# Two heads of layer 0 side by side, their sums on GpSimd, and three steps of layer 1 moved

## The chip, the cores and the metric

One core of a Trainium2 chip runs the whole network in one launch. The metric is the device time of that launch in microseconds, the median of three runs. All data are float32.

## The reference, cut to what matters

Four images of 32 x 32 positions and 384 channels pass through four layers with residual connections. Only the first two matter here (`_gn` is a group norm):

```python
# layer 0, on _gn(x): 6 heads of 64 channels; each query sees its own bias map
q = x @ w_q + b_q                                   # 1024 positions
xs = bilinear sample of x at learned positions      # 1024 samples per head group
k, v = xs @ w_k + b_k, xs @ w_v + b_v
bias = bilinear sample of rpe at (query - position) # 1024 x 1024 per head
attn = softmax(q @ k.T * 64**-0.5 + bias)           # over the 1024 keys
x = x + (attn @ v) @ w_out + b_out

# layer 1, on _gn(x): 12 heads of 32 channels
sim  = sigmoid(beta + alpha * l2norm(xg) @ l2norm(gc).T)  # 1024 x 256 per head
gw   = (sim @ sim.T) * gamma + (1 - gamma)                # 1024 x 1024
attn = softmax(q @ k.T * 32**-0.5) * gw
attn = attn / (attn.sum(keys) + 1e-8)
x = x + (attn @ v) @ Wproj
```

Layers 2 (box filters) and 3 (an attention over 3 x 3 neighbourhoods) follow.

## The kernel before

**Two streams of work.** `Front` computes layer 0 of an image, `Trunk` layers 1 to 3. Both are Python generators that yield weights for the work they have just emitted. `Net.layer3` advances the trunk of image b and, keeping step by these weights (`TRUNK_STEPS` 1109, `FRONT_STEPS` 714), the front of image b + 1. So the front of images 1 to 3 is interleaved with the trunk of images 0 to 2. Image 0's front runs alone at the beginning, and image 3's trunk runs alone at the end. Image 0's heads have code of their own, `heads0`, whose order is pinned by hand.

**Who sets the order.** A scheduling layer takes the emitted instructions, orders each engine's queue by when it expects their inputs, and puts in the waits. Tiles come from pools by tag: `self.wt(shape, tag, bufs)` gives one of `bufs` buffers, and a new tile waits until the last reader of that buffer is done. Engines work through their queues in order, so an instruction that waits holds up all behind it. PSUM has two pools: `bank()` gives one of four tiles of 512 columns, and `big()` one of two tiles of 1024 columns.

**Layer 0's heads, images 1 to 3 (`head0`).** One call handles one head `h` and one half `q` of the queries (512 of them), so there are 12 calls per image. In each, eight blocks `j` of 128 keys are done. For each block:

- an indirect DMA, issued by GpSimd (POOL), gathers a bias window `win` (L830);
- ScalarE (ACT) and VectorE (DVE) interpolate it in y and x: L842, L843, L847, L848, giving `lg`;
- TensorE (PE) multiplies keys and queries (L851). The keys of a head have 64 channels; they lie in `kz`, whose other 64 rows are zero, so that the matmul takes both heads' queries and all 128 rows;
- DVE adds it to `lg` (L852) and keeps a running maximum `rmax` (L855, L857).

Then PE transposes the maxima, DVE reduces them (L868), POOL spreads them on a diagonal (L870), PE broadcasts that (L872) and ACT copies it to `tb` (L876). For each block again, DVE subtracts `tb` (L883), ACT takes the exponential (L884), and PE multiplies with the values `va` into 64 rows of the bank `po`, and with a block of ones into the other 64 rows, which gives the sums (L886). `over_sums` divides after each two heads. The pool of `lg` has 13 buffers of 512 columns.

**Layer 1 (`pair`).** Six calls per image, each for two heads, with eight steps `j` over blocks of 128 keys. In a step:

- POOL scales a slice of the similarities into `sg` (L1492, two buffers);
- PE computes logits with keys and queries of two heads in 64-row tiles (L1509), ACT exponentiates them into `e` (L1517);
- PE multiplies similarities (L1539), or transposes parts that an earlier step had (L1534);
- DVE multiplies this with `e` and sums (L1546); ACT keeps parts for later (L1551);
- PE multiplies with the scaled values (L1481) into `av`.

Beside this runs a pre-pass for the next pair: `sums_step` computes logits in four 32-row tiles (L1382) into two `big` tiles; DVE takes the maximum (L1390) and ACT exponentiates and sums (L1391). `sums_finish` makes the row constants (logarithm on DVE, a transposition on PE, L1416), which are stored and loaded as an extra row of `qa` (`load_lse`). `sims` computes the next pair's similarities (L1429, ACT L1437, DVE L1440). At the end of a pair `av` is copied to `y` (L1569) and stored. The copies of `y` mark the ends of the pairs in the trace.

The core of the emission order in a step, before:

```python
            for h in range(2):          # e of both halves is emitted above
                for r in range(2):      # products, then DVE's multiply (L1546)
                    ...
                if h == 0 and st:
                    for i in (0, 1) if j == 0 else (j + 1,):
                        if i < NJ:
                            self.sums_step(i, st)
                if st and j == NJ - 1:
                    self.sims(h)
            ...
            if st and j == NJ - 2:
                self.sums_finish(p + 1, st)
                self.load_lse(p + 1)
```

Of the kernel before, what the change touches and what calls it, by code (L numbers as in the profile page):

```python
# [20 lines left out]
AF = mybir.ActivationFunctionType  # L21
# [51 lines left out]
class Net:  # L73
# [132 lines left out]
    def scratch(self):  # L206
# [13 lines left out]
        self.k0 = dram("k0", [C, N])  # L220
        self.gcd = dram("gcd", [C, M1])
# [204 lines left out]
class Front(Lane):  # L426


    def layer0(self, b):
        nc, v = self.nc, self.nc.vector  # L430
        with self.scope("l0"):
# [3 lines left out]
            self.kz = [self.wt([P, N], f"kz{r}") for r in range(2)]  # L435
            for r in range(2):
                nc.gpsimd.memset(self.kz[r][GC * (1 - r) : GC * (2 - r), :], 0.0)
            self.va = self.wt([P, NJ, C], "va")
            self.f = self.wt([P, 2, 2, NJ * G], "bias_f")
            self.widx = self.wt([P, 2, NJ * G], "widx", 1, I32)  # L440
            if b == 0:

                self.side = "left"
                with self.scope("l0f"):
                    self.side = "right"
                    self.heads = self.heads0(self.work)
# [9 lines left out]
            with self.scope("l0b"):  # L456
                self.load_keys(0)
                for h in range(G):
                    if h + 1 < G:
                        self.load_keys(h + 1)  # L460
                    for q in range(2):
                        yield from self.head0(h, q)
                    if h % 2:
                        yield from self.over_sums(h // 2)
# [166 lines left out]
    def inputs0(self, b):  # L631
# [145 lines left out]
        va, bv = self.va, self.rows[:, R_BV0 : R_BV0 + C]  # L777
# [3 lines left out]
        def value(j):  # L781
            v.tensor_tensor(va[:, j, :], self.dense_n(xsT, w, j), bv, ALU.add)
# [32 lines left out]
    def head0(self, h, q):  # L815

        nc, v = self.nc, self.nc.vector
        f, kz, va = self.f, self.kz[h % 2], self.va
        k, r0 = h // 2, (h % 2) * GC
        rows = slice(r0, r0 + GC)  # L820
        other = slice(GC - r0, 2 * GC - r0)
        HH, HN = HW // 2, N // 2
        both = self.qpad[:, k, 1 + HH * q : 1 + HH * (q + 1), 1 : 1 + HW]
        queries = both[rows]
        logits = []
        rmax = self.wt([P, HN], "rmax", 2)
        for j in range(NJ):
            c = j * G + h
            win = self.wt([P, (HH + 1) * WROW], "win", 4)
            nc.gpsimd.indirect_dma_start(  # L830
                out=win,
                out_offset=None,
                in_=self.strips[:, :],
                in_offset=bass.IndirectOffsetOnAxis(
                    ap=self.widx[:, q, c : c + 1], axis=0
                ),
            )
            wv = win.rearrange("p (r c) -> p r c", c=WROW)
            sc = lambda i, t: f[:, i, t, c : c + 1]

            z = self.wt([P, HH, HW + 1], "z", 3)
            nc.scalar.activation(z, wv[:, 0:HH, 0 : HW + 1], AF.Copy, scale=sc(1, 1))  # L842
            v.scalar_tensor_tensor(  # L843
                z, wv[:, 1 : HH + 1, 0 : HW + 1], sc(0, 1), z, ALU.mult, ALU.add
            )
            lg = self.wt([P, HH, HW], "lg", 13)
            nc.scalar.activation(lg, z[:, :, 0:HW], AF.Copy, scale=sc(1, 0))  # L847
            v.scalar_tensor_tensor(lg, z[:, :, 1 : HW + 1], sc(0, 0), lg, ALU.mult, ALU.add)  # L848
            lf = lg.rearrange("p y x -> p (y x)")
            ps = self.bank()  # L850
            nc.tensor.matmul(ps, kz[:, j * P : (j + 1) * P], both, start=True, stop=True)  # L851
            v.tensor_tensor(lf, ps, lf, ALU.add)  # L852
            logits.append(lf)
            if j == 1:
                v.tensor_tensor(rmax, logits[0], lf, ALU.max)  # L855
            elif j > 1:
                v.tensor_tensor(rmax, rmax, lf, ALU.max)  # L857
            yield 3


        NI = HN // P
# [19 lines left out]
        for j in range(NJ):  # L881
# [5 lines left out]
            if j % 2:  # L887
                yield 2
# [1038 lines left out]
```

## Time and profile before

| | |
|---|---|
| Time of three runs | 4602.47, 4607.11 and 4614.23 us, median 4607.11 |
| Span of the profiled execution | 4578.1 us, 47313 instructions |
| Outside the span, against the median | 29.0 us |
| Mean granted TensorE clock | 0.948 |
| First `y` copy to the sixth, image 0's trunk | 850.1 to 1459.4 us |
| First `y` copy to the sixth, image 3's trunk | 4042.4 to 4426.9 us |

The profile gives the profiled execution's time as its span, from its first instruction to its last; its device time is not given apart from that, so the difference to the median stands for what lies around the span.

The span is long because everything is done for four images, and because two streams share the engines. A stretch of time in which image 0's trunk runs beside image 1's heads is repeated, nearly alike, for the next two images, some 1112 us later each time (the first `y` copies are at 850.1, 1963.0 and 3075.8 us). The groups of instructions give, for each line, engine and operation, a count of records, the busy time and the mean of one. A float32 matmul leaves two records. The busy time of a group counts overlapping records once, so the busy time divided by the number of matmuls is a better price than the mean duration of a record.

### The profile page before, as it was taken

To read this page: it belongs to the slowest core of one execution; us is meant where nothing else is said; L and a number is where in the kernel's file an instruction comes from. 1 tells how busy PE (TensorE), PEld (TensorE's weight loads), DVE (VectorE), ACT (ScalarE), POOL (GpSimd) and SP (SyncE) were. 2 spreads that over 40 slices of the span, in tenths; PEclk is the share of its full clock that TensorE was granted. 3 is DMA by queue.
4 is the path that set the end of the run, shared out by engine and by line. 5 is a ranking of instruction groups with operands and counts; after the bars stand their busy time and mean duration, and the time that the engine had idled before them with its cause. 6 is when DMAs were issued, how large, how long until landed. Compare 5 with 4: busy or idle time off the path is not lost.

```text
span 4578.1 us, 47313 instructions
## 1 busy us (share of the span) xinstructions
PE 4150.6 (91%) x15896; PEld 1795.0 (39%) x15896; DVE 3138.6 (69%) x5909; ACT 2303.6 (50%) x3633; POOL 972.6 (21%) x994
## 2 busy tenths in 40 slices
PE   5699889999999898999999989899999998999998
PEld 2333334333334443433333444343333335344444
DVE  4599466878787628687878744678786884566654
ACT  2266334667664314465666422456665641555632
POOL 1644123212111104211212110522120211000000
PEclk8799989999999898999999989899999998999998
DMA  6444234212121245321212134432121213311011
GB/s 139 150 144 129 79 125 123 64 52 84 51 59 55 86 114 164 93 55 39 84 50 79 38 105 125 135 103 66 45 71 36 72 38 123 105 32 27 20 41 42
DMA packets 232852, 371.01 MB, mean 81 GB/s; under 512 B 117763, under 2 KB 165728, under 8 KB 232608
## 3 DMA queue, kind: packets, MB, share of 16 engines
q1 hardware_dynamic: 180568, 201.26, 15.4%
q0 software_dynamic: 39936, 145.53, 10.8%
q10 hardware_dynamic: 12104, 21.19, 1.4%
q8 instruction: 126, 2.06, 0.2%
q14 instruction: 118, 0.97, 0.1%
HBM read 287.90 MB, written 80.27 MB: 80 GB/s over the span
## 4 chain that ended last, share of the span: by engine, by line
PE 56%; DVE 14%; ACT 7%; issue 5%; DMA 4%; POOL 2%; SPq 0%; ACTq 0%; DVEq 0%; POOLq 0%
PE bank L1539 13%; PE big L1509 5%; PE big L1382 4%; PE bank L851 4%; PE big L403 4%; PE bank L886 4%; PE bank L417 4%; PE bank L1534 3%; PE bank L1481 3%; DVE nmax L1390 2%; DVE e L1546 2%; PE bank L1219 2%; PE big L666 2%; PE big L1664 1%; POOL gat L738 1%
## 5 line engine op out<-in xcount | busy, mean ns | idle before, releaser
L1539 PE MATMUL bank<-whole,sg 128*128 128x512 f32 (+3 forms) x2304 | 852.5, 505 | 7.0 <-POOL sg L1492 7.0
L1546 DVE SCALAR_TENSOR_TENSOR e<-bank,gam,e 128x512 f32<-128x512 f32 x768 | 561.9, 747 | 349.2 <-PE bank L1539 226.7
L1391 ACT ACTIVATE big<-big,nmax 128x1024 f32<-128x1024 f32 x384 | 417.6, 1087 | 322.3 <-DVE nmax L1390 322.1
L1517 ACT ACTIVATE e<-big 128x1024 f32<-128x1024 f32 x384 | 379.7, 1019 | 363.2 <-PE big L1509 362.1
L1539 PEld LDWEIGHTS bank<-whole,sg 128*128 128x128 f32 x2304 | 403.4, 197 | 369.6 <-issue 281.6
L1390 DVE TENSOR_REDUCE nmax<-big 128x1 f32<-128x1024 f32 x384 | 454.5, 1219 | 76.4 <-PE big L1382 75.9
L830 POOL DMA_INDIRECT win<-strips,widx x288 | 316.2, 1098 | 658.0 <-DVE z L843 391.8
L1492 POOL TENSOR_SCALAR sg<-whole,gam 128x512 f32<-128x512 f32 x192 | 143.7, 750 | 1442.6 <-PE bank L1539 1019.6
L1509 PE MATMUL big<-qa,ka 64*128 64x512 f32 x1536 | 417.8, 630 | 9.7 <-ACT big L1391 9.5
L1382 PE MATMUL big<-k,q 32*128 32x512 f32 x1536 | 327.7, 674 | 82.2 <-ACT big L1391 45.2
L738 POOL DMA_INDIRECT gat<-pairs,sidx x192 | 209.2, 1090 | 378.8 <-DVE ix_gt L519 217.4
L851 PE MATMUL bank<-qpad,kz 128*128 128x512 f32 x576 | 278.8, 613 | 9.4 <-ACT gf L1551 9.4
L886 PE MATMUL bank<-lg,va 128*64 128x512 f32 x576 | 265.6, 605 | 15.0 <-ACT lg L884 14.9
L886 PE MATMUL bank<-lg,ones 128*64 128x512 f32 x576 | 265.0, 605 | 0.0
L848 DVE SCALAR_TENSOR_TENSOR lg<-z,bias_f,lg 128x512 f32<-128x512 f32 x288 | 213.7, 759 | 47.4 <-ACT lg L847 45.7
L1509 PEld LDWEIGHTS big<-qa,ka 64*128 64x128 f32 x1536 | 135.7, 188 | 256.3 <-issue 124.3
L842 ACT ACTIVATE z<-win,bias_f 128x528 f32<-128x528 f32 x288 | 202.9, 735 | 55.4 <-DVE lg L848 34.4
L852 DVE TENSOR_TENSOR lg<-bank,lg 128x512 f32<-128x512 f32 x288 | 192.9, 685 | 49.4 <-PE bank L851 48.1
L883 DVE TENSOR_TENSOR lg<-lg,tb 128x512 f32<-128x512 f32 x288 | 191.5, 710 | 46.9 <-ACT tb L876 46.9
L843 DVE SCALAR_TENSOR_TENSOR z<-win,bias_f,z 128x528 f32<-128x528 f32 x288 | 215.5, 772 | 11.3 <-ACT z L842 9.8
L1481 PE MATMUL bank<-e,vs 128*32 128x512 f32 x1536 | 206.7, 604 | 3.9 <-DVE vs L1475 3.9
L847 ACT ACTIVATE lg<-z,bias_f 128x512 f32<-128x512 f32 x288 | 200.0, 716 | 12.0 <-PE bank L886 6.1
(314 smaller groups left out, 6620.8 us busy)
## 6 DMA issues: line engine op xcount, KB each, us to landing
pairs<-xn SPq DMA_DIRECT2D x64, 192.0 KB
q<-qd SPq DMA_DIRECT2D x48, 256.0 KB
w<-in_gmat SPq DMA_DIRECT2D x16, 576.0 KB
w<-in_w_off SPq DMA_DIRECT2D x12, 576.0 KB
w<-in_Wqkv SPq DMA_DIRECT2D x12, 576.0 KB
a<-in_x SPq DMA_DIRECT2D x16, 384.0 KB
x<-a ACTq DMA_DIRECT2D x4, 1536.0 KB
res<-x SPq DMA_DIRECT2D x12, 512.0 KB
```

Of the source, the lines that this page charges most:

```text
L738: nc.gpsimd.indirect_dma_start(out=gat[:, g].rearrange("p l c -> p (l c)"), out_offset=None, in_=pairs[:, :], in_offset=bass.IndirectOffse ...
L830: nc.gpsimd.indirect_dma_start(out=win, out_offset=None, in_=self.strips[:, :], in_offset=bass.IndirectOffsetOnAxis(ap=self.widx[:, q, c : ...
L851: nc.tensor.matmul(ps, kz[:, j * P : (j + 1) * P], both, start=True, stop=True)
L886: nc.tensor.matmul(po[out, :], w, lf, start=j == 0, stop=j == NJ - 1)
L1382: nc.tensor.matmul(ps[r][:, h * 512 : (h + 1) * 512], self.q4[rows, i * P : (i + 1) * P], self.k4[rows, 0:512], start=True, stop=True,)
L1390: v.tensor_reduce(nmax[:, r, i : i + 1], ps[r], AX.X, ALU.max, negate=True)
L1391: nc.scalar.activation(ps[r], ps[r], AF.Exp, bias=nmax[:, r, i : i + 1], accum_out=den[:, r, i : i + 1],)
L1481: nc.tensor.matmul(av[r0 : r0 + HD1, :], vs[:, r, :], es[h][:, r, :], start=j == 0, stop=j == NJ - 1,)
L1509: nc.tensor.matmul(ps[:, r, :], ka[rows, j * P : (j + 1) * P], qa[rows, cols], start=True, stop=True,)
L1517: nc.scalar.activation(e, ps, AF.Exp)
L1539: nc.tensor.matmul(ps[:, (mid - i0) * P :], sg[:, r, m, :], sim[:, h, r, m, (mid - i0) * P :], start=m == 0, stop=m == 1,)
L1546: v.scalar_tensor_tensor(e[:, r, :], ps, self.gam[:, 1:2], e[:, r, :], ALU.add, ALU.mult, accum_out=tot[:, r, h : h + 1],)
```

## The change

Line numbers in this section are given for the kernel before.

**Layer 0, images 1 to 3.** `two_heads(k, q)` takes the place of two calls of `head0`. It handles heads 2k and 2k + 1 together. Keys of both heads are loaded as one tile of 128 rows without zeros. Their logits are two matmuls of 64 rows each, into the two halves of one `big` tile. The four interpolation instructions stay 512 wide for each head; the addition, maximum, subtraction and exponential become 1024 wide. Values of two heads go into the two 64-row halves of `po`, each with its own exponentials. The sums over the blocks are additions on POOL into `acc`, and two matmuls with ones follow at the end. Values no longer stay in SBUF for these images: they are stored to DRAM in `inputs0` and loaded for two heads at a time. Keys and values have one buffer each. The weights yielded add up to the same.

**Layer 1.** `sims` uses four tiles of 32 rows, for which `load_groups` loads `xg` and `gc` in another layout, without zero fills. The pre-pass takes two rounds in each of steps 0 and 1 and one in each of steps 2 to 5. It is queued on PE behind products of its step (`issue_after`: issue order alone, no wait). `sums_finish` is split: `sums_log` is emitted at the end of step 5, `sums_row` (PE, ACT, store) and `load_lse` in step 6. `sims(0)` moves to step 6, `sims(1)` stays in step 7. `y` uses a buffer of the tag `sg`.

```diff
+    def two_heads(self, k, q):
+        queries = self.qpad[:, k, 1 + HH * q : 1 + HH * (q + 1), 1 : 1 + HW]
+        half = lambda r: slice(r * GC, (r + 1) * GC)
+        rmax = self.wt([P, 2, HN], "rmax", 2)
         for j in range(NJ):
-            lg = self.wt([P, HH, HW], "lg", 13)
-            ps = self.bank()
-            nc.tensor.matmul(ps, kz[:, j * P : (j + 1) * P], both, start=True, stop=True)
-            v.tensor_tensor(lf, ps, lf, ALU.add)
+            lg = self.wt([P, 2, HN], "lg", 9)
+            ps = self.big()
+            for r in range(2):
+                nc.tensor.matmul(
+                    ps[:, r * HN : (r + 1) * HN],
+                    keys[half(r), j * P : (j + 1) * P],
+                    queries[half(r)],
+                    start=True,
+                    stop=True,
+                )
+            for r in range(2):
...
+                if r == 0:
+                    yield 3
+            v.tensor_tensor(flat(lg), ps, flat(lg), ALU.add)
...
             yield 3
+        if q and k + 1 < KC:
+            self.keys = self.pair_keys(k + 1)
...
         po = self.bank()
+        acc = self.wt([P, 2, HN], "rmax", 2)
         for j in range(NJ):
-            lf = logits[j]
-            v.tensor_tensor(lf, lf, tb, ALU.subtract)
-            nc.scalar.activation(lf, lf, AF.Exp)
-            for out, w in ((rows, va[:, j, h * GC : (h + 1) * GC]), (other, self.ones[:, 0:GC])):
-                nc.tensor.matmul(po[out, :], w, lf, start=j == 0, stop=j == NJ - 1)
-            if j % 2:
-                yield 2
+            lg = logits[j]
+            v.tensor_tensor(flat(lg), flat(lg), tb, ALU.subtract)
+            nc.scalar.activation(flat(lg), flat(lg), AF.Exp)
+            for r in range(2):
+                nc.tensor.matmul(
+                    po[half(r), :], vals[:, j, half(r)], lg[:, r], start=j == 0, stop=j == NJ - 1
+                )
+            if j:
+                first = logits[0] if j == 1 else acc
+                nc.gpsimd.tensor_tensor(flat(acc), flat(first), flat(lg), ALU.add)
+            yield 2
+        if q and k + 1 < KC:
+            self.vals = self.pair_values(k + 1)
...
+        for r in range(2):
+            nc.tensor.matmul(
+                ps[half(r), :], self.ones[:, 0:GC], acc[:, r], start=True, stop=True
+            )
...
         def value(j):
-            v.tensor_tensor(va[:, j, :], self.dense_n(xsT, w, j), bv, ALU.add)
+            out = self.va[:, j, :] if b == 0 else self.wt([P, C], "xn", 2)
+            v.tensor_tensor(out, self.dense_n(xsT, w, j), bv, ALU.add)
+            if b > 0:
+                nc.sync.dma_start(self.v0[j * P : (j + 1) * P, :], out)
...
     def load_groups(self, p):
-        for r in range(2):
-            c0, r0 = (2 * p + r) * HD1, 64 * r
-            nc.sync.dma_start(self.xg[r0 : r0 + HD1, :], self.xgd[c0 : c0 + HD1, :])
-            nc.sync.dma_start(self.gc[r0 : r0 + HD1, :], self.gcd[c0 : c0 + HD1, :])
+        ch = slice(p * 64, (p + 1) * 64)
+        for m in range(2):
+            rows = slice(64 * m, 64 * (m + 1))
+            nc.sync.dma_start(self.xg[rows, :], self.xgd[ch, :])
+            nc.sync.dma_start(self.gc[rows, :], self.gcd[ch, m * P : (m + 1) * P])
...
     def sims(self, h):
+        ps = [self.big().rearrange("p (r n) -> p r n", r=2) for _ in range(2)]
         for m in range(2):
-            ps = self.big().rearrange("p (r n) -> p r n", r=2)
             for r in range(2):
-                rows = slice(64 * r, 64 * r + 64)
+                rows = slice(64 * m + 32 * r, 64 * m + 32 * r + 32)
...
+            parts = [(0, 0), (0, 1), (1, 0), (1, 1)]
+            split = 2 if j < NJ // 2 else 3
+            for h, r in parts[:split]:
+                last = product(h, r)
+            with self.tc.issue_after(last):
+                if st and j < 2:
+                    self.sums_step(2 * j, st)
+                elif st and j < 6:
+                    self.sums_step(j + 2, st)
+                elif st and j == 6:
+                    self.sums_row(p + 1, logs)
+                    self.load_lse(p + 1)
+                    self.sims(0)
+            for h, r in parts[split:]:
+                last = product(h, r)
+            with self.tc.issue_after(last):
+                if st and j < 2:
+                    self.sums_step(2 * j + 1, st)
+                elif st and j == 7:
+                    self.sims(1)
             if late:
                 values(*late.pop())
             late.append((j, es, tot))
-            if st and j == NJ - 2:
-                self.sums_finish(p + 1, st)
-                self.load_lse(p + 1)
+            if st and j == 5:
+                logs = self.sums_log(st)
                 if p + 2 < NH1 // 2:
                     self.load_sums(p + 2)
...
-        y = self.wt([P, 512], "y")
+        y = self.wt([P, 512], "sg", 2)
```

## The prediction, made before the changed kernel ran

> **What bounds the kernel now.** I read the busy shares first, then two stretches that do the same trunk work with and without the heads of layer 0 beside it, then the PE timeline inside one stretch, then single groups.
>
> ```profile
> PE 4150.6 (91%) x15896; PEld 1795.0 (39%) x15896; DVE 3138.6 (69%) x5909; ACT 2303.6 (50%) x3633; POOL 972.6 (21%) x994
> ...
> 850.10:1352.40 502.30, 468.60 (x1875) 185.34 (x1875) 399.95 (x774) 323.20 (x515) 96.62 (x99) 0.98 0.20 57
> 4042.40:4364.20 321.80, 313.30 (x1446) 134.50 (x1448) 200.39 (x461) 192.88 (x305) 22.13 (x32) 0.99 0.10 26
> ...
> 200.00:400.00 200.00, 189.23 (x585) 71.02 (x583) 185.25 (x268) 133.42 (x224) 102.61 (x106) 1.00 0.54 161
> ```
>
> The rows by stretch give length, then busy time of PE, PEld, DVE, ACT and POOL, then clock. The first two each hold four head pairs of layer 1, cut at the copies of `y` (L1569). With heads beside it a pair takes 502.3/4 = 125.6 us, alone 321.8/4 = 80.5. PE is busy for 117.2 and 78.3 of those: the heads add 45.1 us of time and 38.9 of PE work. So PE sets the pace, at nearly full clock, and PE work taken out of the heads should come off the time until the next engine stops it. DVE is next: 400.0/4 = 100.0 of 125.6, 80%. The last row, where image 0's heads run alone, shows DVE at its fullest in this trace, 92.6%.
>
> ```profile
> 1004.81 1.14 PE L1382 MATMUL big<-k,q 32*128 32x512 f32 x8
> 1005.88 3.70 PE L1539 MATMUL bank<-whole,sg 128*128 128x512 f32 x8
> 1009.51 1.07 PE L1481 MATMUL bank<-e,vs 128*32 128x512 f32 x8
> 1010.51 2.85 PE L851 MATMUL bank<-qpad,kz 128*128 128x512 f32 x6
> 1013.29 1.99 PE L1509 MATMUL big<-qa,ka 64*128 64x512 f32 x8
> ```
>
> Two records are one matmul. Four full ones (L1539) take 3.70 us; four of 64 rows (L1509) take 1.99, so they run in twos; four of 32 rows (L1382) or of 32 columns with four different inputs (L1481) take 1.1, all at once.
>
> ```profile
> L1509 PE MATMUL big<-qa,ka 64*128 64x512 f32 x1536 | 417.8, 630 | 9.7 <-ACT big L1391 9.5 <-ACT whole L1437 0.2
> L1382 PE MATMUL big<-k,q 32*128 32x512 f32 x1536 | 327.7, 674 | 82.2 <-ACT big L1391 45.2 <-ACT e L1517 36.8
> L851 PE MATMUL bank<-qpad,kz 128*128 128x512 f32 x576 | 278.8, 613 | 9.4 <-ACT gf L1551 9.4
> L886 PE MATMUL bank<-lg,va 128*64 128x512 f32 x576 | 265.6, 605 | 15.0 <-ACT lg L884 14.9
> L886 PE MATMUL bank<-lg,ones 128*64 128x512 f32 x576 | 265.0, 605 | 0.0
> L1429 PE MATMUL big<-xg,gc 64*128 64x512 f32 x384 | 106.2, 621 | 11.7 <-ACT e L1517 8.7 <-ACT whole L1437 3.0
> ...
> L870 POOL TENSOR_TENSOR diag<-ident,top 128x512 f32<-128x512 f32 x36 | 40.6, 1129 | 168.4 <-DVE top L868 168.2
> L1686 POOL TENSOR_TENSOR whole<-sq,whole 128x1024 f32<-128x1024 f32 x12 | 29.0, 2417 | 188.4 <-ACT sq L1680 188.4
> ```
>
> The two L886 groups overlay each other (the sums already run beside the values), so they cost about 265 us together, not 530. L1686 is the operation that is added: a 128x1024 sum on POOL, 2.417 us.
>
> **The change part by part**, per unit of two heads and half the queries. There are 18 units, 6 for each of images 1 to 3; image 0 keeps its own code. Front and trunk advance by the same steps as before, so one unit still goes with one pair.
>
> *Logits.* 16 full matmuls at 278.8/288 = 0.968 us, 15.5, become 8 side-by-side twos at 417.8/384 = 1.088, 8.7: 6.8 us of PE saved.
>
> *Values and sums.* 16 overlaid twos at 265.6/288 = 0.922, 14.7, become 8 such twos, 7.4, and one more two for the sums, 0.9: 6.4 saved. Maxima and diagonals do the same PE work in wider instructions. In the new instruction order PE changes the shape of its tiles 1524 times, before 1530; a change costs about 0.2 us (1.07 for one round of four against 3.70/4 = 0.925), so nothing is added there.
>
> *Similarities.* Per pair 4 twos at 106.2/96 = 1.106, 4.4 us, become 2 rounds of four at 1.07: 2.3 saved.
>
> *Pre-pass.* A round of L1382 should take 1.07 us. In the groups of the two stretches it takes 43.6/32 = 1.36 without heads and 56.9/32 = 1.78 with them, since half of the round waits for a PSUM tile that ACT still holds; behind the products, as it is queued now, PE has other work while ACT frees it. At best (1.78 - 1.07) x 8 = 5.7 us a pair, below nothing if DVE and ACT get it later than they do now; I take 3.0. Where no heads run, 0.8. The row constants move from the end of step 6 of a pair to after it: PE waits there for DVE 24.2 us in 24 pairs (L1416), 1.0 a pair, which goes. The logarithms stay on DVE, one step earlier. `load_sums` for the pair after next is issued a step earlier on SP, so nothing is late.
>
> *DVE.* Per unit 16 adds at 0.670 become 8 at about 1.22 (the 1024-wide reduction L1390 takes 1.219), the subtractions and 14 maxima alike: 3.3 us saved. The 1024-wide POOL sums are new: 7 x 2.417 = 16.9 us. POOL has the room, 96.6/4 = 24 of 125.6 us. What matters is what they hold up. The rows that bear on it:
>
> ```profile
> L843 DVE SCALAR_TENSOR_TENSOR z<-win,bias_f,z x288: 737/761/1885, 780.6 to 3679.5; 128x528 f32<-128x528 f32 x144
> L967 DVE SCALAR_TENSOR_TENSOR z<-win,bias_f,z x96: 715/762/1423, 187.4 to 481.1; 128x528 f32<-128x528 f32 x96
> L883 DVE TENSOR_TENSOR lg<-lg,tb x288: 636/684/1754, 855.5 to 3760.1; 128x512 f32<-128x512 f32 x144
> ```
>
> Medians of 761, 762 and 684 ns stand beside maxima of 1885, 1423 and 1754: now and then one waits. In image 0, where POOL does 45.3 us of two-input work (`dg` 32.4, `diag` 12.9), L967 has a mean of 949, so (949 - 762) x 96 = 18.0 us are lost, and L1051, mean 813 against 685, loses 6.1: 24 of 45, about half. In the units L843 and L883 lose (772 - 761) x 288 + (710 - 684) x 288 = 10.7 us against 40.6 of `diag`, a quarter. The Trainium skill (SBUF — State Buffer, "Who interferes with whom") speaks against this change: a DVE instruction with two SBUF inputs and a GpSimd one that reads SBUF lock each other out for the whole instruction. By that rule at its worst all 16.9 us land on DVE: 100.0 - 3.3 + 16.9 = 113.6 a pair. By the rows a quarter to a half does; I take 40%, 6.7: 103.4. The ends, 97 and 114, are kept for the range.
>
> *POOL's queue.* `sg` (PE needs it each step) and the next `win` gathers stand behind the sums, which wait for ACT's exponentials. In the new order up to six sums stand in a row, 14.5 us, longer than one step of a pair (12.7 us at 1000 us). `sg` runs up to two steps ahead (POOL waits 1019.6 us for PE there), which covers nearly all; if that cover is gone, up to 4 us a pair. Also `y` now takes an `sg` buffer until its store has landed. I take 2.0 for both.
>
> *The rest* costs nothing while covered. 24 stores of values at 192 KB and 9 loads of them on SP land before the heads' second phase, some 50 us later. 9 key loads wait for the last logits and have the values' phase, tens of us, before the next logits; SP's later loads queue behind them but are issued a step ahead. `xg` is loaded twice over (48 DMAs of double size, DMA share 0.20). 16 fewer zero fills. ACT saves about 3 us a unit, 64% busy. Uncovered, a key or value load is 512 KB, some 4 us at the 130 GB/s of the first 200 us, 18 times: 72 us.
>
> *Sum for a pair with heads:* PE 117.2 - 6.8 - 6.4 - 2.3 - 3.0 - 1.0 = 97.7, with today's idle 8.4 it would be 106. DVE needs 103.4 and has never been above 92.6% here: 111.7. So DVE takes over. With 2.0 for POOL: 113.7, 11.9 less than 125.6. Five units of each image run beside pairs: 15 x 11.9 = 179. The sixth runs beside layers 2 and 3 (1459 to 1541: PE 95% busy, DVE 78%): 13.2 of PE work, of which 10 come through, 30. The last image's six pairs without heads: 2.3 + 0.8 + 1.0 = 4.1 each, 25. Sum 234. Against the span of 4578.1 this gives 4344; 29.0 us lie between span and median (4607.1), so 4373 before losses elsewhere. One is likely: only 9 logit buffers of double width against 13 single ones, which lets the next unit start one tile ahead instead of two and a half. That is 1.5 tiles x 2.2 us of DVE work, 3 us for half of the units, about 27. Forecast 4400.
>
> **The rivals.** *The PE gain comes through whole* (8%): the sums fall where DVE works on PSUM (L1546, L1390), pairs take 106: 15 x 19.6 + 40 + 25 = 359, 4250. Against it: DVE would be 95% busy.
>
> *The locks by the rule* (17%): DVE 113.6/0.926 = 122.7 and 2.0: 0.9 x 15 + 55 = 69, less 27 for the buffers: 4565.
>
> *Slower: PSUM's two large tiles become the bound* (15%). The head logits move from the four banks to the two `big` tiles. Per pair these are claimed 36 times now (16 L1509, 16 L1382, 4 L1429), then 47 times. From the timeline L1509 holds one 2.3 us, L1382 4.2, similarities 2.6, the three others of a unit about 3.2: 124 us of 2 x 125.6. The page TensorEngine Tiling (Array Packing), "PSUM Bottleneck", warns that tiling speeds up TensorE and not the emptying; no row of this trace shows that limit reached. Eight logit tiles at h us each, with tiles 80% used, break even at (124 + 8h)/1.6 = 125.6, h = 9.6 us. A tile needs 1.09 + 1.22 us and waits for two chains of ACT and DVE work on `z`; if PE issues it 9 us ahead of them, this decides. At h = 12 a pair takes 137.5: +12 x 15 - 55 = +125, 4732. For it: both tiles stand in the order with head logits at places, PE then waiting for DVE. Against it: `z` needs no PSUM and is mostly ordered ahead.
>
> *It doesn't do what it says* (2%): the twos run one after the other, nothing is gained, 4607. L1509 and L1481 speak against it.
>
> **How the numbers follow.** About 0.3%, 14 us, is what a measurement can tell from no change. Forecast 58%, its own range 4320 to 4500. Faster: 57 of it, 8, and 15 of the locks' 17: 0.80. Within: 0.05. Slower: the PSUM rival, 0.15. The range of 4300 to 4615 leaves out about 5% below and 15% above.
>
> **What would show it.** Right: 288 key matmuls at 1.09 a two, pairs near 114 us by the `y` copies, DVE above 88% there, sums of 2.4 us on POOL with DVE's subtractions lengthened beside them, and no PE wait at the row constants. Wrong: waits of PE for `big` released by DVE, `sg` named before L1539, or pairs still at 125.

## The result, and the profile after

The changed kernel takes 4756.91 us (median of 4 runs, 4752.58 to 4762.86), the kernel before on the same chip 4610.67 (4 runs, 4602.47 to 4616.73). The ratio is 1.0324, with an interval of 1.0305 to 1.0344: 146 us slower, where 4400 was forecast and 4615 was the upper end of the range. The profiled execution has a span of 4750.8 us and a mean granted clock of 0.911. Below, 1% of the kernel before is put at 46 us.

In every later execution for which both are known, device time lies 1.7 to 3.1 us above the span. So the 29.0 us between span and median before are, for the most part, not time around the span: the profiled execution was a faster one. Medians of the kernel before went from 4578 to 4611 us with the chip. A ratio below is always taken on one chip; a price that is the difference of two chips' ratios takes it that a ratio is the same on both. Stretches that are compared across two traces can differ by up to 0.7% for this reason alone, some 4 us in 502.

First the busy shares of the changed kernel, then its stretches between copies of `y` (L1637): length, busy time of PE, PEld, DVE, ACT and POOL, and the clock. The first holds four pairs with heads, the second four pairs without, the third runs from the sixth `y` copy of image 0 to the first of image 1.

```profile
PE 4040.2 (85%) x15392; PEld 1708.5 (36%) x15392; DVE 3277.2 (69%) x5477; ACT 2272.9 (48%) x3438; POOL 1338.8 (28%) x1098
```

```profile
862.90:1391.10 528.20, 444.83 (x1762) 164.46 (x1764) 420.51 (x670) 307.42 (x460) 172.21 (x121) 0.93 0.20 55
4228.50:4535.60 307.10, 303.51 (x1448) 127.75 (x1444) 199.58 (x460) 193.00 (x306) 22.24 (x32) 1.00 0.12 31
1502.30:2041.00 538.70, 455.10 (x1640) 214.79 (x1642) 320.88 (x518) 193.99 (x293) 134.74 (x113) 0.87 0.37 111
```

PE lost 110 us of work in the whole run, and the time rose. A pair with heads now takes 528.2/4 = 132.05 us (125.6 before), with PE busy for 111.2 (117.2) and DVE for 105.1 (100.0). DVE's share is still 80%: no engine is near full, and PE, DVE and ACT all stand idle for longer. A pair without heads takes 76.8 us (80.45). The third stretch has grown from 503.6 us to 538.7; the stretch of all pairs, from the first `y` copy to the sixth, from 609.3 to 639.4. That makes 65 us per image, about half of it where the sixth unit runs beside layers 2 and 3.

The groups that the change touches: out<-in and shapes, count, then busy time and mean ns of one record, then idle time ahead of them.

```profile
L1562 PE MATMUL big<-qa,ka 64*128 64x512 f32 x1536 | 475.4, 676 | 114.2 <-DVE lg L875 77.8 <-ACT big L1438 23.6 <-ACT e L1570 8.7
L844 PE MATMUL big<-qpad,keys 64*128 64x512 f32 x576 | 167.2, 667 | 51.9 <-ACT big L1438 36.8 <-ACT whole L1490 12.7 <-issue 0.9
L921 PE MATMUL bank<-lg,vals 128*64 128x512 f32 x576 | 146.9, 636 | 32.3 <-ACT lg L919 32.0
L918 DVE TENSOR_TENSOR lg<-lg,tb 128x1024 f32<-128x1024 f32 x144 | 277.8, 1962 | 106.1 <-ACT tb L910 106.1
```

The key matmuls (L844) cost 167.2/144 = 1.16 us a two. The layer-1 logits (L1562, L1509 before) have grown from 417.8 to 475.4 us for the same work and wait for the large tiles. The subtraction of the maxima (L918) takes 1.96 us in the mean. Single instructions tell more than means. Each line has minimum, median and maximum in ns:

```profile
L926 POOL TENSOR_TENSOR rmax<-rmax,lg x108: 2340/3208/3402, 920.6 to 3932.8; 128x1024 f32<-128x1024 f32 x108
...
L918 DVE TENSOR_TENSOR lg<-lg,tb x144: 1210/1225/3397, 913.7 to 3917.2; 128x1024 f32<-128x1024 f32 x144
...
L872 DVE SCALAR_TENSOR_TENSOR lg<-z,bias_f,lg x288: 729/748/2837, 800.2 to 3837.4; 128x512 f32<-128x512 f32 x144
...
L875 DVE TENSOR_TENSOR lg<-big,lg x144: 1170/1218/1227, 839.7 to 3892.2; 128x1024 f32<-128x1024 f32 x144
...
L1599 DVE SCALAR_TENSOR_TENSOR e<-bank,gam,e x768: 733/748/756, 731.2 to 4595.0; 128x512 f32<-128x512 f32 x192
```

A sum on POOL takes 2.34 us undisturbed and mostly 3.2. The subtraction takes 1.21 undisturbed and up to 3.40, the second interpolation (L872) up to 2.84; both read two operands in SBUF. The addition of the logits (L875) and layer 1's multiply (L1599) read one operand in PSUM and stay within 50 ns of their medians. Start and end times of single records say it more sharply. Of the 144 subtractions, 58 start while a sum runs on POOL. These 58 and no others are lengthened, and each ends 1.08 to 1.09 us after that sum has ended. So a subtraction that comes second stands until the sum is done. This is the rule of the Trainium skill (SBUF — State Buffer, "Who interferes with whom") as the prediction quoted it, now in this case's numbers; it is called the lock below. Two waits of PE stand out:

```profile
PEld big L1562 <- DVE lg L875: 159.3, 111, 5.3
...
PEld bank L1592 <- DVE e L1599: 105.0, 52, 9.9
```

The first is PE waiting for a large tile that DVE has not yet emptied, the sign that the prediction named for its PSUM rival. Before, the head logits lay in banks and this wait did not exist. The second is PE waiting for layer 1's multiply. It was 27.7 us before (L1539), is 49.6 in the run without sums below, and 105.0 here, where the multiply stands behind DVE's lengthened instructions.

### The profile page after: what moved, and what is told of

The parts are those of the page before. It is cut to its first block, busy times and chain, and to the rows that moved or that the text cites. A ratio compares the mean times of both kernels' runs of the same rounds, so it can differ in the third digit from the quotient of the medians.

```text
span 4750.8 us, 45871 instructions
## 1 busy us (share of the span) xinstructions
PE 4040.2 (85%) x15392; PEld 1708.5 (36%) x15392; DVE 3277.2 (69%) x5477; ACT 2272.9 (48%) x3438; POOL 1338.8 (28%) x1098
## 5 line engine op out<-in xcount | busy, mean ns | idle before, releaser
L1592 PE MATMUL bank<-whole,sg 128*128 128x512 f32 (+3 forms) x2304 | 880.7, 513 | 60.8 <-DVE e L1599 58.5
L1599 DVE SCALAR_TENSOR_TENSOR e<-bank,gam,e 128x512 f32<-128x512 f32 x768 | 559.4, 747 | 303.5 <-PE bank L1592 184.9
L1562 PE MATMUL big<-qa,ka 64*128 64x512 f32 x1536 | 475.4, 676 | 114.2 <-DVE lg L875 77.8
L1592 PEld LDWEIGHTS bank<-whole,sg 128*128 128x128 f32 x2304 | 401.6, 199 | 447.7 <-issue 297.1
L918 DVE TENSOR_TENSOR lg<-lg,tb 128x1024 f32<-128x1024 f32 x144 | 277.8, 1962 | 106.1 <-ACT tb L910 106.1
L1429 PE MATMUL big<-k,q 32*128 32x512 f32 x1536 | 297.9, 657 | 38.5 <-ACT big L1438 19.0
L926 POOL TENSOR_TENSOR rmax<-rmax,lg 128x1024 f32<-128x1024 f32 x108 | 316.2, 2928 | 32.8 <-ACT lg L919 26.2
L1562 PEld LDWEIGHTS big<-qa,ka 64*128 64x128 f32 x1536 | 139.2, 199 | 417.8 <-DVE lg L875 159.3
L1534 PE MATMUL bank<-e,vs 128*32 128x512 f32 x1536 | 234.5, 615 | 40.9 <-DVE vs L1528 40.7
L872 DVE SCALAR_TENSOR_TENSOR lg<-z,bias_f,lg 128x512 f32<-128x512 f32 x288 | 255.1, 898 | 18.5 <-ACT lg L871 15.1
L867 DVE SCALAR_TENSOR_TENSOR z<-win,bias_f,z 128x528 f32<-128x528 f32 x288 | 216.9, 771 | 16.8 <-ACT z L866 16.2
L844 PE MATMUL big<-qpad,keys 64*128 64x512 f32 x576 | 167.2, 667 | 51.9 <-ACT big L1438 36.8
L1604 ACT COPY gn<-bank 128x128 f32<-128x128 f32 (+2 forms) x288 | 106.3, 370 | 217.7 <-DVE e L1599 217.6
L919 ACT ACTIVATE lg<-lg 128x1024 f32<-128x1024 f32 x144 | 149.8, 1055 | 104.4 <-DVE lg L918 103.2
```

Of the source, the lines that this page charges most:

```text
L872: v.scalar_tensor_tensor(lr, z[:, :, 1 : HW + 1], sc(0, 0), lr, ALU.mult, ALU.add)
L918: v.tensor_tensor(flat(lg), flat(lg), tb, ALU.subtract)
L926: nc.gpsimd.tensor_tensor(flat(acc), flat(first), flat(lg), ALU.add)
L1429: nc.tensor.matmul(ps[r][:, h * 512 : (h + 1) * 512], self.q4[rows, i * P : (i + 1) * P], self.k4[rows, 0:512], start=True, stop=True,)
L1534: nc.tensor.matmul(av[r0 : r0 + HD1, :], vs[:, r, :], es[h][:, r, :], start=j == 0, stop=j == NJ - 1,)
L1562: nc.tensor.matmul(ps[:, r, :], ka[rows, j * P : (j + 1) * P], qa[rows, cols], start=True, stop=True,)
```

## The experiments

Theory A: the locks between POOL's sums and DVE carry the loss. Rival B: PSUM's large tiles. Others came up on the way. Runs that are told together shared a chip and its runs of the kernel before.

**Parts of the change.** The first kernel has only layer 1's part. The second leaves out the sums, the third keeps them and puts the logits in two banks, the fourth does both.

```diff
# no sums
-            if j:
-                first = logits[0] if j == 1 else acc
-                nc.gpsimd.tensor_tensor(flat(acc), flat(first), flat(lg), ALU.add)
-                 ps[half(r), :], self.ones[:, 0:GC], acc[:, r], start=True, stop=True
+                 ps[half(r), :], self.ones[:, 0:GC], logits[NJ - 1][:, r], start=True, stop=True
# banks
-            ps = self.big()
+            ps = [self.bank() for _ in range(2)]
-            v.tensor_tensor(flat(lg), ps, flat(lg), ALU.add)
+            for r in range(2):
+                v.tensor_tensor(lg[:, r], ps[r], lg[:, r], ALU.add)
```

> Layer 0 as before, layer 1 as after: the moved pre-pass, row constants, four-tile similarities and the shared buffer of y alone. If layer 1 is innocent: pairs without heads 76.8 us as in after (80.5 before), six of them 22 us, and as much again or more beside heads, so 4520 to 4590. If the new order of layer 1 is what costs beside the heads: above 4611, in the direction of 4757.

> After, with the 126 sums on GpSimd taken out; the denominators are those of the last block of keys alone (that part of the softmax is left out). Locks theory (a sum on GpSimd shuts out DVE's instructions with two SBUF inputs): the 1024-wide subtraction goes from a mean of 1962 ns back to about 1225, the second interpolation from 898 to about 750, some 150 us of DVE, and the time falls by 120 to 250: 4510 to 4640. Tile theory (PE waits for the two large PSUM tiles that the head logits hold): nothing of this changes, 4720 or more. Depth theory (nine wide logit buffers are too few): a part, since the buffers come free earlier, 4680 to 4740.

> After, with the two heads' logits in two banks of 512 columns in place of one large tile, and two additions of 512 in place of one of 1024. Tile theory: PE's waits for DVE's addition at the layer 1 logits (237 us in after) go, 4600 to 4670. Locks theory: no gain, 16 additions at 0.68 in place of 8 at 1.22 add 1.2 us a unit, 22 in all: 4740 to 4790. If banks are as scarce as large tiles, it gets slower than after too.

> Both edits together: no sums on GpSimd (denominators of the last block alone) and logits in two banks. If locks and tiles each carry a part, the two gains add: 4380 to 4520. If the locks carry all, it equals the run without the sums; if the tiles carry all, it equals the run with logits in banks.

| kernel | us | ratio to before (interval) |
|---|---|---|
| layer 1's part alone | 4527.85 | 0.989 (0.987 to 0.991) |
| no sums | 4533.21 | 0.9894 (0.9874 to 0.9915) |
| logits in banks | 4670.78 | 1.0196 (1.0175 to 1.0217) |
| no sums, in banks | 4476.71 | 0.9782 (0.976 to 0.9804) |

Layer 1's part is a gain of 1.1%, some 51 us: a pair without heads takes 76.8 us, one with heads 123.9. The whole loss is layer 0's. The sums cost 1.0324 - 0.9894 = 4.3%, some 198 us (4.1% with the logits in banks). The large tiles cost 1.3% with the sums and 1.1% without, 59 and 52 us. The two prices add up: neither hides behind the other. Without the sums the subtraction is back at its own time:

```profile
L917 DVE TENSOR_TENSOR lg<-lg,tb 128x1024 f32<-128x1024 f32 x144 | 170.5, 1218 | 105.8 <-ACT tb L910 105.8
```

The four pairs with heads, in the run of layer 1's part, in the one without sums, and in the one that has banks too:

```profile
842.90:1338.40 495.50, 465.38 (x1876) 181.98 (x1876) 398.00 (x775) 321.37 (x516) 99.07 (x99) 0.97 0.21 59
```

```profile
851.70:1341.80 490.10, 435.10 (x1765) 163.11 (x1766) 378.94 (x670) 305.79 (x461) 91.01 (x93) 0.96 0.21 59
```

```profile
853.60:1328.20 474.60, 427.72 (x1762) 167.16 (x1762) 379.48 (x700) 304.56 (x458) 89.66 (x92) 0.94 0.21 60
```

A pair takes 123.9, 122.5 and 118.7 us. So two heads side by side are worth about 1.1% over layer 1's part alone, but the large tiles take just that back: the run without sums only ties with layer 1's part.

**What in a sum costs.** Three replacements of the sum, and its move to DVE.

```diff
# sums of ready tiles
-                nc.gpsimd.tensor_tensor(flat(acc), flat(first), flat(lg), ALU.add)
+                nc.gpsimd.tensor_tensor(flat(acc), tb, tb, ALU.add)
# half width
+                nc.gpsimd.tensor_tensor(acc[:, 0], first[:, 0], lg[:, 0], ALU.add)
# writes
+                nc.gpsimd.memset(flat(acc), 1.0)
+                nc.gpsimd.memset(flat(acc), 0.0)
# on VectorE, with the logits in banks
+                v.tensor_tensor(flat(acc), flat(first), flat(lg), ALU.add)
```

> The changed kernel with each of the 126 GpSimd sums replaced by a 128x1024 addition of the maxima's tile to itself, whose result nobody reads: same place in the program, same size, two SBUF operands, but no wait for an exponential, no chain from sum to sum, and no logit tile held for it. Left out: the denominators' sums (they are taken from the last block alone). Theory A, the lock: what costs is GpSimd's reading of SBUF beside VectorE's two-operand instructions, so nearly the whole cost of the sums (4.3 per cent between the run without them, 0.989, and the changed kernel, 1.032) comes back: 1.02 to 1.04, with the subtraction of the maxima again near 1.95 us in the mean against 1.22 without sums. Theory B, the waits: what costs is that GpSimd's queue stands behind the exponentials, or that tiles come free late: 0.985 to 1.00, the subtraction near 1.3.

> The changed kernel with each GpSimd sum over the first head's 512 columns alone; the second head's denominators are taken from the first head's. Waits, tile lifetimes and the place in the queue are the changed kernel's, only the length of a sum halves (2.93 to about 1.4 us). Theory A, the lock, which costs by the length of the overlap: about half of the 4.3 per cent goes, 1.005 to 1.015, with the subtraction near 1.5 us. Theory B, waits and late release: nearly all of it stays, 1.025 to 1.035.

> The changed kernel with each GpSimd sum replaced by two GpSimd fills of the 128x1024 accumulator with a constant (a fill of 32x1024 takes 1.03 to 1.15 us in the trace, so two are some 2.2 us, against 2.4 for an undisturbed sum): GpSimd is busy as long and its queue stands as long, and it writes SBUF, but reads none of it. Left out: the denominators' sums (the last block alone). Theory A, a lock on reading: no cost, 0.985 to 0.995, VectorE's subtraction near 1.22 us. If any GpSimd work beside VectorE blocks it, or the occupied queue costs (the merges and gathers behind it): 1.01 to 1.035.

> The changed kernel with the seven sums of a unit on VectorE (128x1024, two SBUF operands, about 1.21 us each by the maxima's rows: 8.5 us a unit) and the logits in two one-bank tiles. Nothing is left out. Against the run with banks and no sums (0.978; VectorE 379.5 of 474.6 us, 80 per cent, over the pairs with heads) VectorE gets 8.5 us per pair more: 94.9 + 8.5 = 103.4 of a pair that stood at 118.7. If VectorE's time hides as it does at 80 per cent: 0.985 to 0.99, a tie with or a small gain on the run of layer 1's part alone (0.989). If VectorE's chain carries it: 8.5 us on each of 18 units, 3.3 per cent, 1.01. On GpSimd in banks it was 1.020: less than that shows that the sum costs more there than on the engine it was to relieve.

| kernel | us | ratio to before (interval) | subtraction, mean ns |
|---|---|---|---|
| sums of ready tiles | 4726.89 | 1.0247 (1.0208 to 1.0285) | 2072 |
| half width | 4646.11 | 1.0084 (1.0055 to 1.0113) | 1525 |
| writes | 4572.12 | 0.9913 (0.9885 to 0.9942) | 1217 |
| on VectorE, in banks | 4552.70 | 0.9877 (0.9845 to 0.9908) | 1216 |

Sums that wait for nothing cost 3.5%, nearly as much as the real ones; half the width costs 1.9%, a little under half; and fills in place of sums cost 0.2%, which is within the intervals. The groups of the first, and of the writes:

```profile
L918 DVE TENSOR_TENSOR lg<-lg,tb 128x1024 f32<-128x1024 f32 x144 | 293.9, 2072 | 106.9 <-ACT tb L910 106.9
...
L925 POOL TENSOR_TENSOR rmax<-tb 128x1024 f32<-128x1024 f32 x126 | 347.3, 2756 | 51.4 <-ACT tb L910 43.2
```

```profile
L918 DVE TENSOR_TENSOR lg<-lg,tb 128x1024 f32<-128x1024 f32 x144 | 170.4, 1217 | 106.0 <-ACT tb L910 106.0
...
L925 POOL MEMSET rmax<- 128x1024 f32 x126 | 123.1, 977 | 4.8
```

The trace of the fills shows a limit of that run. A fill waits for no exponential, so POOL did the fills early: those of a unit ended 31 to 67 us before its first subtraction, and none of the 144 subtractions ran beside one. So the 1217 ns say nothing of writes. What does is the second interpolation (L872), which reads two operands in SBUF. Of its 288 instructions 61 ran beside a fill, 55 of them at their usual time, and the longest took 1.17 us, as in the run without sums; beside sums it reached 2.84.

```profile
L872 DVE SCALAR_TENSOR_TENSOR lg<-z,bias_f,lg x288: 725/743/1174, 804.3 to 3679.3; 128x512 f32<-128x512 f32 x144
```

What lengthens DVE is that POOL reads SBUF while DVE reads two operands there, by the length of the read. The waits for exponentials and the late release of `lg` are not needed for it: with ready tiles they are gone, and some 80% of the price is still there. The tables of groups show the lengthening of all DVE instructions against the run without sums (count times the difference of means): 211 us in the changed kernel, 158 with ready tiles, 88 at half width. They cost 198, 163 and 88 us. So the price of the sums is about as large as the lengthening, though DVE was busy for only 80%. In all three runs, though, POOL's queue is held at the same place too, and no run here holds it there without a lock. The sums on DVE itself added 3212.3 - 3077.5 = 135 us of DVE's busy time to the run with banks and no sums, and cost 0.95%, 44 us: a third.

**Why the price is so high.** First guess: the place decides, since the subtraction lies on a unit's chain from maximum to exponential. So the same filler of DVE work was put ahead of the exponential and behind it (on the run without sums).

```diff
+            v.tensor_scalar(flat(lg), flat(lg), 1.0, None, ALU.mult)     # ahead
             nc.scalar.activation(flat(lg), flat(lg), AF.Exp)
+            v.tensor_scalar(flat(acc), flat(lg), 1.0, None, ALU.mult)    # or behind the matmuls
```

> The run without GpSimd sums (0.989), with one VectorE instruction more per block: the subtracted logit tile times 1.0, in place, ahead of its exponential (one SBUF operand, about 0.71 us by the 128x1024 scalar row, 144 of them: 102 us, 2.2 per cent). Left out: the denominators' sums (the last block alone). It sets by VectorE's own work what the lock did to the subtraction (0.74 us longer in the mean), at the same place. Theory C, the place decides (VectorE's time between the maxima and the exponential lies on the chain of a unit): nearly all of it comes through, 1.007 to 1.013. Theory D, VectorE time costs about a third anywhere, as the VectorE sums did (140 us of it for 0.95 per cent), and the lock has a cost of another kind: 0.994 to 0.999.

> The same filler of 0.71 us, 144 times, behind the exponential in place of the sum, into a tile that nobody reads. Left out: the denominators' sums (the last block alone). Theory C: it lies aside of the chain and costs about a third, 0.994 to 0.999, less than the filler ahead of the exponential by over 0.8 per cent. Theory D: the same as that run.

Ahead: 4585.96 us, 1.0002 (0.999 to 1.0013). Behind: 4576.79 us, 0.9988 (0.998 to 0.9997). The filler took 0.69 us each and added 78 and 79 us to DVE's busy time; it cost 1.1% and 0.9%, 50 and 43 us. The place makes 0.14%, not the 0.8% of theory C, which falls. At both places DVE's time costs some 55 to 64% of itself. With the filler ahead, the four pairs:

```profile
850.40:1352.33 501.93, 442.23 (x1765) 163.99 (x1766) 397.30 (x702) 306.64 (x461) 90.23 (x93) 0.95 0.21 58
```

11.8 us longer than without it, for 18.4 more of DVE. In the changed kernel it was 38.1 for 41.6. Two things could make that difference: lumps (a lengthened instruction stands up to 2.2 us longer), or POOL's own queue, held 2.93 us by a sum where two fills held it for 1.95.

```diff
# longer writes: a third memset
+                nc.gpsimd.memset(flat(acc), 1.0)
# lumps
+            if j in (1, 3, 5, 7):
+                for _ in range(5):
+                    v.tensor_scalar(flat(lg), flat(lg), 1.0, None, ALU.mult)
```

> The run with GpSimd fills in place of the sums (two of 0.98 us each, 0.991), with three fills: 2.93 us of GpSimd for each sum, just what a sum took in the changed kernel, with no read of SBUF. Left out: the denominators' sums (the last block alone). If part of the sums' price is GpSimd's queue, held longer than two fills hold it (window gathers and the merges behind it): 1.002 or more. If GpSimd's occupation is free: 0.988 to 0.996, and the price is VectorE's alone.

> The run without GpSimd sums (0.989), with VectorE fillers in lumps: five in a row (0.69 us each, 3.4 us by their durations, about 2.7 us of added busy time as the evenly spread filler showed 0.54 each) ahead of every second exponential, 360 in all, so that VectorE's busy time grows by some 195 us, as much as the lock added (205). Left out: the denominators' sums (the last block alone). If lumps are paid in full, one for one: 1.028 to 1.036, as the changed kernel. If half of it stays hidden, as with the even filler (50 of 79 us of busy time): 1.010 to 1.017, and the lock's full price has another reason.

Longer writes: 4588.33 us, 0.9977 (0.9965 to 0.9989), 0.8% above the run without sums, 38 us. Lumps: 4675.99 us, 1.0169 (1.0139 to 1.02), 2.75%, 127 us, with these busy shares:

```profile
PE 4026.7 (86%) x15392; PEld 1696.1 (36%) x15392; DVE 3276.9 (70%) x5837; ACT 2275.0 (49%) x3438; POOL 976.2 (21%) x972
```

DVE's busy time is that of the changed kernel to 0.3 us, 205 above the run without sums, and it costs 127/205 = 62%, the rate of the even filler. So lumps alone don't bring the full price. An account of the 198 us could read: DVE's time at the rate of the lumps 127, POOL held as long as by the sums 38, together 165. The last 33 us stay open, within about 20 us of uncertainty from the four ratios' intervals.

The traces show two reasons to take this account as an estimate only. First, the three fills too ran early: those of a unit ended 10 to 59 us before its first subtraction, so their 38 us are the price of a queue that is held at another time. Second, the scheduling layer plans with a filler, but not with a lock. In the changed kernel and with ready tiles all of DVE's instructions stand in the same order as without sums. With the fillers taken out of the sequence, 4754 (ahead), 4811 (behind) and 4082 (lumps) of some 5480 stand at the same place in it. PE's waits fit this: it waits for layer 1's multiply (weight loads of L1592 and its like) 49.6 us without sums, 105.0 in the changed kernel and 113.7 with ready tiles, but 38.4 with the filler ahead and 35.3 with lumps. So part of the lock's higher price may be that nothing was ordered around it. No run separates this from POOL's queue, and the cause of what lies above 62% stays open.

A hint, not tested: in the third stretch the locks added 15.5 us of DVE and 19.2 of time per image, for instance 3.3 to 3.4 in place of 1.2 to 1.3 us on layer 2's and 3's lone DVE instructions. In the timeline of the changed kernel:

```profile
1575.45 3.42 DVE L1719 TENSOR_TENSOR t<-sq 128x1088 f32<-128x1088 f32 x1
...
1582.20 3.27 DVE L1721 TENSOR_TENSOR whole<-whole,sq 128x1024 f32<-128x1024 f32 x1
...
1587.81 3.36 DVE L1759 TENSOR_TENSOR dn<-dn,xp 128x1024 f32<-128x1024 f32 x1
```

**PE's price, and the depth of the tiles.** These two ran with the evenly spread fillers: the sums as matmuls with ones, logits in banks, and the kernel before with 9 logit tiles.

```diff
+            for r in range(2):
+                nc.tensor.matmul(
+                    ps[half(r), :], self.ones[:, 0:GC], lg[:, r], start=j == 0, stop=j == NJ - 1
+                )
# the kernel before
-            lg = self.wt([P, HH, HW], "lg", 13)
+            lg = self.wt([P, HH, HW], "lg", 9)
```

> The changed kernel with the logits in two one-bank tiles and each block's sum on TensorE: two more matmuls with ones per block, into a second bank held as long as that of the values. Nothing is left out. Against the run with banks and no sums (0.978) 288 x 1.09 us less the final pair of each unit: 8 x 1.09 - 1.09 = 7.6 us of TensorE per unit, 137 us over 18, 3.0 per cent. TensorE is 90 per cent busy there: if it is the bound, 1.003 to 1.010, and the sums are cheaper on VectorE (0.988). If the second held bank starves the two that are left, above 1.015.

> The kernel before, with 9 logit tiles of one head in place of 13: the depth that the changed kernel has, by itself (one tile beyond the eight of a unit). The forecast put 27 us on it, 0.6 per cent: 1.004 to 1.008. If depth costs nothing, 0.998 to 1.002, and the gap between what TensorE lost in work and what the run with neither sums nor large tiles gained lies elsewhere; if it is a main cost, over 1.012.

Sums on PE: 4538.25 us, 0.9902 (0.9878 to 0.9926). PE's busy time is 4056.0 us against 3966.1 without sums, and these 90 us cost 1.2%, 55 us: 61%, not the whole that a bound engine would ask, so the expected 1.003 to 1.010 missed. What the second held bank costs is in these 55 us. Nine tiles: 4615.75 us, 1.0081 (1.0049 to 1.0112), 37 us for the depth. The pairs don't show it (608.4 us from the first `y` copy to the sixth, 609.3 before); the third stretch does, 517.9 against 503.6.

Three kernels that leave nothing out beat the kernel before and the changed one: layer 1's part alone (0.989), two heads in banks with the sums on DVE (0.9877) and with the sums on PE (0.9902). Their intervals overlap; which is best stays open.

## Why the prediction was wrong

The forecast lay 207 us below its own 4607; measured were 146 above, 353 us apart. Two steps of the sum failed, and both rest on one idea: that a single engine bounds a pair, and that time of the others is free.

*The larger step* is "with today's idle 8.4 it would be 106". It takes PE's saved work off the pair one for one. Without any price for the sums it gives 294 + 40 + 25 - 27 = 332 us. The run without sums gained 49. A pair took 122.5 us there, with PE busy for 108.8 and idle for 13.8, and 118.7, 106.9 and 11.8 with banks. So some 283 of the 353 us were lost here. Known by runs are layer 1's part, 51 us in place of 119; the large tiles, 52; the depth of `lg`, 10 more than the forecast's 27. About 150 us are left. An estimate says how they go together. From layer 1's part alone to the run with neither sums nor large tiles, PE's busy time fell by 4115.4 - 3966.1 = 149 us, where 18 x 13.2 = 238 were forecast. At the 61% that PE's time was seen to cost, 149 bring 91. Less 37 for the depth, that is 54, and 50 were measured. That PE's time is worth 61% when it is taken away, too, was not tried.

*The smaller step* is "DVE needs 103.4 and has never been above 92.6% here: 111.7. So DVE takes over." It let DVE's added time lie hidden until DVE was nearly full. With POOL's 2.0 it put the sums at 332 - 207 = 125 us; they cost 198. At 80% busy, DVE's added time was paid in part in every run: a third for sums on DVE, 55 to 64% for fillers, and for the locks 76% if POOL's queue took 38 us, more if it took less. So the lock by the rule's rival, 4565, was too low as well: it used the same step.

*The lock's size* was put at 40% of 16.9 us a unit, 6.7. It was 211/18 = 11.7, or 69%. DVE's 103.4 a pair still came near the measured 105.1, by two errors that cancel in part: without sums DVE stood at 94.7 where 96.7 was expected, and the locks added 10.4. The quarter to a half was misread. It sets the lengthening of L843, L883 and L967 against `diag` and `dg`, but by their times these mostly met others. Of the 21 lengthened L883 of before, 15 start while POOL scales `sg` (L1492), 3 while it does L1686, and none beside `diag`; 29 of the 35 lengthened L967 start while POOL issues a window's DMA. The new sums run beside eight subtractions in a row, and 58 of 144 of these begin during one.

*POOL's queue*, 2.0 us a pair: with fills as long as the sums 38/18 = 2.1. The number agrees; since the fills held the queue at another time, that is in part luck.

*PE's savings* against before, by groups: logits 278.8 - 167.2 = 111.6, 6.2 a unit (forecast 6.8); values and sums 265.6 - 146.9 - 18.8 = 99.9, 5.5 (6.4); similarities 106.2 - 71.9 = 34.3, 1.4 a pair (2.3); pre-pass 327.7 - 297.9 = 29.8, 1.2 a pair (3.0). The first two came near, the last two brought about half. What was left out is that other work got longer: layer 1's logits by 57.6 us, 2.4 a pair. So PE's busy time fell to 111.2 in a pair with heads, and to 106.9 without sums and with banks, where the sum had 97.7. Part of that may be the clock, 0.98 before and 0.93 after.

*Layer 1's part* without heads: 4.1 a pair forecast, 3.7 measured. With heads 6.3 forecast (similarities, pre-pass, row constants), and 125.6 - 123.9 = 1.7 in the run of that part alone.

*The sixth unit* was to bring 10 us an image through. The stretch that holds it became 35 us longer; 19 of these go with the sums, and nine tiles alone cost 14 there.

*The PSUM rival* (15%) had a true mechanism, and its sign stood in the trace after, 159.3 us of weight loads waiting for `lg` (L875). The prediction says that no row of before shows PE held up by the emptying of PSUM; its own row of L1382 does, 82.2 us idle for ACT. But the rival measured 52 to 59 us, 3 a unit, and did not decide by itself: without the sums the kernel ends at a tie with layer 1's part. It was forecast at 4732, near the measured 4757, by luck: most of the loss has the other cause.

Of the signs: sums at 2.4 us failed (2.93), DVE above 88% failed (80%), pairs near 114 failed (132), and key matmuls took 1.16 in place of 1.09. Subtractions lengthened beside the sums came true. The wait at the row constants shrank and did not end: PE itself stood 24.2 us for DVE there before (L1416) and 9.0 after.

## What to carry to other kernels

Do not count on hiding work on an engine because it is 80% busy, and do not take saved work of the busiest engine off the time one for one. Put a filler of known length there and read what a microsecond of it costs (here 55 to 64% on DVE, 61% on PE; real sums on DVE cost a third). Check in the trace that the filler runs where it was meant to, and whether the rest was reordered around it. GpSimd additions out of SBUF beside VectorE's two-operand work were the dearest place for a sum: with the logits in banks the same sums cost 191 us there, 44 on VectorE and 55 on TensorE.

## What was not expected of the hardware

- A GpSimd sum of 128x1024 out of SBUF takes 2.34 us alone and 3.2 in the median beside VectorE's subtractions, a fill of the same size 0.98 us. A subtraction that starts during a sum ends 1.08 us after it, in all 58 cases.
- Fills are not free for every VectorE instruction: of the 16 scalar operations on `whole` (TENSOR_SCALAR 128x1024, L1493, one operand) that ran beside a fill, 15 were lengthened, to 1.10 us in the median against 0.69.
- With more idle time of PE in the pairs with heads (7% before, 16% after) its granted clock there was lower, 0.93 in place of 0.98, and the same products of layer 1 took 883.6 us in place of 854.4. So waits may make the matmuls longer too; this was not tried by itself.
- The first interpolation (L867) reads two SBUF operands too, yet its longest took 1.30 us against a median of 0.76, while L872 reached 2.84. By their times none of the 288 L867 ran beside a sum, and 24 of the L872 did. So L867 was spared by its place in the order.
